# Two attentions, a norm and an MLP on one core: an earlier handed-over projection, and value weights scaled in place of the values

## The chip, the cores and the metric

The kernel runs on one core of one Trainium2 chip. The metric is the device time of one execution in microseconds (us); the time of before is a median of three runs. The engines are called as in the profile: PE is TensorE's matmul and PEld its weight load, DVE is VectorE, ACT is ScalarE, POOL is GpSimd, SP is the engine whose queue issues most of the transfers. PSUM, where matmuls write, has eight banks of 512 fp32 values for each of 128 partitions.

## The reference

Sixteen images with 256 channels and 32 x 32 positions pass through two layers. All is fp32.

```python
# layer 0: 4 heads of 64
xs = x.reshape(B, C, S).transpose(0, 2, 1)
q, k, v = jnp.split((xs @ w_proj + b_proj).reshape(B, S, 4, 192), 3, axis=-1)
attn = softmax(einsum('bihd,bjhd->bijh', q, k) * 64 ** -0.5, axis=2)
x = einsum('bijh,bjhd->bihd', attn, v).reshape(B, S, 256) @ w_out + b_out + xs
...
# layer 1: 8 heads of 32
def attention(x, qkv_w, proj_w, proj_b, phys_bias):
    ...
    attn = softmax(einsum('bhnd,bhmd->bhnm', q, k) * 32 ** -0.5 + phys_bias)
    out = einsum('bhnm,bhmd->bhnd', attn, v)
    return out @ proj_w.T + proj_b
x = x + attention(group_norm(x, gn1_w, gn1_b), qkv_w, proj_w, proj_b, phys_bias)
h = gelu(mlp_w1 @ group_norm(x, gn2_w, gn2_b) + mlp_b1, approximate=False)
return x + mlp_w2 @ h + mlp_b2
```

The group norm has 32 groups of 8 channels. `phys_bias` is one number per head, so it multiplies the exponentials of a head by exp(bias).

## The kernel before

**Stages.** The loop over the 16 images (`b`, called batch) runs, for each, a first attention (`attention_a`, names ending in `_a`), the first group norm (`g`), a second attention (`attention_b`, names ending in `_b`), the second group norm (`h`) and the MLP. The stages of neighbouring images are laid into each other by hand: the first half of the MLP of image b-1 (`hidden`) stands behind the first attention of image b; the second half (`outputs`) and the query, key and value products of image b+1 are pieces (`fill`) between the steps of the second attention of image b. The first image has no MLP beside it, and the last one no next image.

**Order.** The program is written as one sequence. `run` goes through a stage that is a generator, and calls `later.tick()` at each of its steps; `later.after(n, fn)` puts `fn` n ticks ahead. From this sequence the framework builds one queue per engine. An engine takes its queue in order; the order on VectorE and ScalarE isn't that of the source text in all places, since the framework may put an operation ahead of others that it finds independent.

**First attention.** Four items (two halves `t` of the positions, two channel halves `c`) of eight key blocks make 32 units. A unit n has the scores `s_a` (L390, into a double-bank slot), the exponential `e_a` on ScalarE (L398), and two units later the weighted sum `acc_a` (L411) and, from an item's second key block on, one addition `es_a` on VectorE (L423) for the denominators. At an item's end ScalarE and VectorE empty `acc_a` (L427, L428). Of the eight banks six form three slots 0, 1, 2, given out by `wide` to the least recently used first; two are single (`bank` 0 and 1). An item of odd number keeps its `acc_a` in slot 2, and `kept` holds that slot back from `wide`; an item of even number uses the single banks.

`normalise(t)` follows some ticks behind the second item of a half: it takes a slot, multiplies the sums by ones (`den_a`, L442), copies the result (L350), spreads it over the partitions by a DMA, inverts it (L359), sends it back by DMAs and has `res_a` multiplied (L468).

**What is handed over.** The last projection `j` of the second attention of image b-1 is not issued there but kept in `handed`. In `attention_a` of image b it is issued at the end of `normalise(0)`, between the scores of units 18 and 19 (numbered from 0):

```python
            kept.discard(2)
            if t == 0 and handed:
                handed.pop()()
```

`out_proj` writes `j` into a slot, adds it into `x` (L663), and takes statistics (L666). `group_norm` follows through `later`: `means` (L711, L713), three ticks on `variances` (a tiny matmul `gm_h`, L703 or L336, and L720 to L726), two ticks on `apply` (`gv_h`, L733, a power on GpSimd at L734, L736 to L740, and four steps `gn_h` at L746), and then, one tick each, five sums of the MLP's input (L875 to L879). The statistics of the second norm in a 64-column tiling are read by two halves of the partitions; the two tiny matmuls write the two banks of one slot.

**End of the first attention.** Behind the last unit come the first projection half `o` in bank 0, the denominators of the second half (`normalise(1)`) and `o` in bank 1, then `hidden` (L898, L911, L923 to L954), in the middle of which the other `o` and the first norm stand.

**Second attention.** Before it, five pieces: four query/key tiles `qk_b` and the first value tile `v_b`, each into a slot through `single` (a bank if `aside` names one); ScalarE copies `qk_b` (L770). VectorE copies `v_b` while it multiplies by `eones`, exp(bias) for each column (L793). Its 16 steps have two key blocks each: scores (L524), of which the first two tiles go to bank 0 and 1, five exponentials (L539), additions on VectorE (L555), and the weighted sum of the step before in bank 0 (L576). The second value tile goes to bank 0 in the first step's fill (`early`).

**Start of the program.** SP's queue loads the first half of `x`, its second half, then `wo`, `wq` (the weights of the second attention's q, k and v), `wpj`, and the next `x`. ScalarE makes exp(bias) (L205) and VectorE spreads it to `eones` (L206). A bias tile `bqk` is turned by TensorE and copied by VectorE (L1058); the copies of the first attention's q and k on ScalarE (L772) need it.

Of the kernel before, what the change touches and what calls it, by code (L numbers as in the profile page):

```python
# [14 lines left out]
P = 128  # L15
# [3 lines left out]
HEADS1, D1 = 8, 32  # L19
# [35 lines left out]
def kernel(  # L55
# [21 lines left out]
    nc = tc.nc  # L77
# [126 lines left out]
    def exp_bias():  # L204
        nc.scalar.activation(ebias, pb, AF.Exp)  # L205
        nc.vector.tensor_copy(eones, ebias.unsqueeze(2).to_broadcast([P, HEADS1, D1]))  # L206

    bvo = const.tile([P, CC], F32, name="bvo")
    m2b2 = const.tile([P, CC], F32, name="m2b2")

# [2 lines left out]
    with ExitStack() as first:  # L213
        first_pass(
            first, tc, x, out,
            dict(
                wp=wp, bqk=bqk, pb=pb, bo=bo, g1w=g1w, g1b=g1b, g2w=g2w,
                g2b=g2b, pjb=pjb, m1b=m1b, m2b=m2b, wo=wo, wq=wq, wpj=wpj,
                m2b2=m2b2, gavg=gavg, mhalf=mhalf, ones=ones, eones=eones,
                bvo=bvo, at_start=at_start, load_rest=load_rest, exp_bias=exp_bias,  # L220
                make_blocks=make_blocks,
                in_range=in_range,
            ),
        )

    good = nc.values_load(in_range[0:1, 0:1], min_val=0, max_val=1)
    with tc.If(good == 0):
        with ExitStack() as again:
            general_pass(
                again, tc, x, out,  # L230
                dict(
                    wp=wp, bqk=bqk, pb=pb, bo=bo, g1w=g1w, g1b=g1b, g2w=g2w,
                    g2b=g2b, pjb=pjb, m1b=m1b, m2b=m2b, wo=wo, wq=wq, wpj=wpj,
                    mlp_w1T=mlp_w1T, mlp_w2T=mlp_w2T, gavg=gavg, mhalf=mhalf, b_proj=b_proj,
                ),
            )


def first_pass(ctx, tc, x, out, k):
# [136 lines left out]
    def attention_a(b, qT, kT, v, project):  # L376
# [57 lines left out]

        def normalise(t):
            half = TB // 2
            den = wide(f"den_{key}_{t}")[:, 0, :]
            for c in range(CC):
                for g in range(2):
                    for h in range(2):  # L440
                        j = (2 * g + h) * 32
                        nc.tensor.matmul(  # L442
                            den[j : j + 32, c * half : (c + 1) * half],
                            k["ones"],
                            sums[t * CC + c][:, g, h * half : (h + 1) * half],
                            start=True,
                            stop=True,
                        )

            home = act.tile([P, CC, S], F32, tag="k1", name=f"d_{key}_{t}")  # L450
            denominators(
                f"{key}_{t}", den, home[:, 1, :TB], home[:, 0, : CC * TB],
                (2, 5) if t < NT - 1 else (1, 1),
                lambda full: scale(t, full),
            )


            kept.discard(2)
            if t == 0 and handed:
                handed.pop()()  # L460

        def scale(t, full):
            r = res[:, :, t * TB : (t + 1) * TB]
# [10 lines left out]
        for n, u in enumerate(units):  # L474
            pending.append(scores(*u))
            if n == len(units) - 1:
                break
            if n >= lag:
                weigh(*pending.pop(0))
            yield  # L480
        while pending:
            weigh(*pending.pop(0))
# [207 lines left out]
    def group_norm(key, src, stats, gw, gb, tag, out_tile, wait, then=None):  # L690
        st = {}

        def averages(name, src):
            if cols[0] == P:
                ps = bank(name, 1)
                product(ps[:, :CC], k["gavg"], src, start=True, stop=True)
                return [(slice(0, P), ps[:, :CC])]
            ps = wide(name)  # L700
            halves = [slice(h, h + HALF) for h in range(0, P, HALF)]
            for n, sl in enumerate(halves):
                nc.tensor.matmul(  # L703
                    ps[sl, n, :CC], k["gavg"][sl, sl], src[sl], start=True, stop=True
                )
            return [(sl, ps[sl, n, :CC]) for n, sl in enumerate(halves)]

        def means():
            mv = small.tile([P, CC, 2], F32, tag="mv", name=f"mv_{key}")
            for cc in range(CC):  # L710
                nc.vector.bn_aggr(mv[:, cc, :], stats[:, cc].rearrange("p t k -> p (t k)"))  # L711
            mean_c = small.tile([P, CC], F32, tag="mean_c", name=f"mean_c_{key}")
            nc.vector.tensor_copy(mean_c, mv[:, :, 0])  # L713
            st.update(mv=mv, mean_c=mean_c)
            later.after(wait, variances)

        def variances():
            mean = small.tile([P, CC], F32, tag="mean", name=f"mean_{key}")
            for sl, ps in averages(f"gm_{key}", st["mean_c"]):
                nc.vector.tensor_copy(mean[sl], ps)  # L720

            dv = small.tile([P, CC], F32, tag="dv", name=f"dv_{key}")
            nc.vector.tensor_sub(dv, st["mean_c"], mean)
            nc.vector.tensor_mul(dv, dv, dv)
            tv = small.tile([P, CC], F32, tag="tv", name=f"tv_{key}")
            nc.vector.tensor_add(tv, dv, st["mv"][:, :, 1])  # L726
            st.update(mean=mean, tv=tv)
            later.after(1 if cols[0] == P else 2, apply)

        def apply():  # L730
            rstd = small.tile([P, CC], F32, tag="rstd", name=f"rstd_{key}")
            for sl, ps in averages(f"gv_{key}", st["tv"]):
                nc.vector.tensor_scalar(rstd[sl], ps, EPS, None, ALU.add)  # L733
            nc.gpsimd.tensor_tensor(rstd, rstd, k["mhalf"], ALU.pow)  # L734
            a = small.tile([P, CC], F32, tag="ga", name=f"ga_{key}")
            nc.vector.tensor_mul(a, rstd, gw)  # L736
            ma = small.tile([P, CC], F32, tag="gma", name=f"gma_{key}")
            nc.vector.tensor_mul(ma, st["mean"], a)
            c = small.tile([P, CC], F32, tag="gc", name=f"gc_{key}")
            nc.vector.tensor_sub(c, gb, ma)  # L740
            y = act.tile([P, CC, S], F32, tag=tag, name=f"gn_{key}")
            out_tile.append(y)
            for t in range(NT):
                sl = slice(t * TB, (t + 1) * TB)
                for cc in range(CC):
                    nc.vector.tensor_scalar(  # L746
                        y[:, cc, sl], src[:, cc, sl],
                        a[:, cc : cc + 1], c[:, cc : cc + 1], ALU.mult, ALU.add,
                    )
            if then:  # L750
                then(y)

        means()

    def qkv(key, D, src, weights, b_qk, v_scale, qT, kT, v_dst):
# [18 lines left out]
        def v(n):  # L776
            ps = single(f"v_{key}_{n}")
            for i in range(2):
                sb = 2 * n + i
                for cc in range(CC):  # L780
                    product(
                        ps[:, i * C : (i + 1) * C],
                        src[:, cc, sb * P : (sb + 1) * P],
                        weights(cc, 2),
                        start=(cc == 0),
                        stop=(cc == CC - 1),
                    )
            d = v_dst()[:, 2 * n : 2 * n + 2]
            ps = ps.rearrange("p (b h d) -> p b h d", b=2, d=D)
            if v_scale is None:  # L790
                nc.scalar.copy(d, ps)
            else:
                nc.vector.tensor_mul(  # L793
                    d, ps, v_scale.unsqueeze(1).to_broadcast([P, 2, C // D, D])
                )

        return (
            [
# [6 lines left out]
    def qkv_0(b, xb):  # L805
# [5 lines left out]
        def v():  # L811
# [4 lines left out]
        return (q, kk, v), qkv(  # L816
            f"a{b}", D0, xb,
            lambda cc, which: k["wp"][:, cc, which].rearrange("p h d -> p (h d)"),
            k["bqk"], None, q, kk, v,
        )  # L820

    def qkv_1(b, xn):
# [3 lines left out]
        return (q, kk, v), qkv(  # L826
            f"b{b}", D1, xn,
            lambda cc, which: k["wq"][:, cc, which * C : (which + 1) * C],
            None, k["eones"], q, kk, lambda: v,
        )  # L830

    def attention_0(b, qkv_tiles, xb, norm):
# [251 lines left out]
        nc.vector.tensor_add(k["bvo"], ps[:, :CC], k["bo"])  # L1084

    later.after(2, fold_bias)
    hidden, outputs = [], []
    last = NT * CC * SB // 2 - 1
    for b in range(B):
# [25 lines left out]

        run_pieces(qk[:n] + v[:1])
        def early(piece):
            aside.append(0)  # L1120
# [56 lines left out]
def general_pass(ctx, tc, x, out, k):  # L1177
# [23 lines left out]
    nc.gpsimd.dma_start(w1, k["mlp_w1T"].rearrange("(c p) n -> p c n", p=P))  # L1201
    w2 = act.tile([P, HC, C], F32, tag="w2", name="g_w2")
    nc.gpsimd.dma_start(w2, k["mlp_w2T"].rearrange("(c p) n -> p c n", p=P))
    pbs = small.tile([P, HEADS1], F32, name="pbs", bufs=1)
    nc.vector.tensor_scalar(pbs, k["pb"], float(D1) ** 0.5, None, ALU.mult)

# [260 lines left out]
```

## Time and profile before

| what | value |
|---|---|
| median of 3 runs | 3700.42 us (3700.16 to 3700.57) |
| span of the profiled execution | 3698.8 us (no other timing of this execution is given) |
| TensorE matmul busy | 3644.9 us, 99% |
| VectorE busy | 2688.2 us, 73% |
| ScalarE busy | 2118.4 us, 57% |
| GpSimd busy | 121.1 us, 3% |
| granted TensorE clock, mean | 0.999 |

The span runs from the first to the last instruction. Busy time is the union of an engine's instructions. Matmul records overlap, since four 32-column tiles or the like run at once, and their ends are modelled; so the distance between the starts of two groups says more than a group's length. A row of the timeline has start, length, engine, line, operation, tiles and count, and in brackets the idle time of the engine ahead of it with what ended it.

### The profile page before, as it was taken

Reading aid. Unit: us, or ns where it says so; the run is one execution under the profiler, and the core shown is the slowest. Engines: PE = TensorE matmul, PEld = TensorE weight load, DVE = VectorE, ACT = ScalarE, POOL = GpSimd, SP = SyncE. Lnnn points to the kernel's source line nnn. Section 1 sums busy time; section 2 is a strip of 40 time slices with the busy share of each in tenths; the row PEclk is TensorE's granted clock in tenths of the full one; section 3 lists DMA queues with packets and bytes.
Section 4 is the critical chain, followed back from the end, with each engine's and each line's share of the span. In section 5 each row is a group of like instructions: output and inputs, shape, how many; then the busy total and the mean of one; then the engine's idle time right before and its main releaser. Section 6 shows DMA issues by size and latency. Waiting matters only on the chain.

```text
span 3698.8 us, 79399 instructions
## 1 busy us (share of the span) xinstructions
PE 3644.9 (99%) x34221; PEld 1290.8 (35%) x34221; DVE 2688.2 (73%) x3486; ACT 2118.4 (57%) x2768; POOL 121.1 (3%) x266
## 2 busy tenths in 40 slices
PE   9999999999999999999999999999999999999999
PEld 4333333333333333333333333333333333333333
DVE  4686767767677776777777777787777877677777
ACT  4665646556565665646656465564655656556572
POOL 3000000000000000000000000000000000000000
PEclk9999999999999999999999999999999999999999
DMA  4000110101101011010110101001010010101100
GB/s 146 11 16 30 53 33 13 50 30 53 33 14 50 30 53 33 19 49 28 50 33 19 50 27 50 32 19 50 27 56 27 23 46 33 50 27 42 36 28 27
DMA packets 66548, 138.35 MB, mean 37 GB/s; under 512 B 35630, under 2 KB 36398, under 8 KB 61966
## 3 DMA queue, kind: packets, MB, share of 16 engines
q1 hardware_dynamic: 63116, 126.64, 10.7%
q8 instruction: 270, 4.42, 0.5%
q0 software_dynamic: 1328, 6.17, 0.5%
q14 instruction: 88, 0.72, 0.1%
q10 hardware_dynamic: 1746, 0.40, 0.1%
HBM read 111.17 MB, written 21.23 MB: 36 GB/s over the span
## 4 chain that ended last, share of the span: by engine, by line
PE 81%; DVE 14%; issue 3%; DMA 1%; ACT 1%; POOL 1%; SPq 0%; DVEq 0%; ACTq 0%
PE s_b L524 12%; PE acc_b L576 12%; PE m L336 10%; PE s_a L390 9%; PE acc_a L411 8%; PE m L898 6%; PE qk_a L336 6%; PE qk_b L336 5%; DVE es_a L423 4%; PE v_a L336 3%; PE j L336 3%; PE v_b L336 2%; PE den_b L598 1%; DVE g L954 1%; DVE es_b L555 1%
## 5 line engine op out<-in xcount | busy, mean ns | idle before, releaser
L539 ACT ACTIVATE e_b<-s_b 128x1024 f32<-128x1024 f32 (+1 forms) x1280 | 983.0, 864 | 151.0 <-PE s_b L524 151.0
L555 DVE TENSOR_TENSOR es_b<-es_b,e_b 128x1024 f32<-128x1024 f32 x768 | 899.1, 1218 | 217.3 <-ACT e_b L539 217.2
L398 ACT ACTIVATE e_a<-s_a 128x1024 f32<-128x1024 f32 x512 | 521.3, 1025 | 360.1 <-PE s_a L390 345.7
L524 PE MATMUL s_b<-q,k 32*64 32x512 f32 x8192 | 526.9, 601 | 9.8 <-DVE v L793 7.0
L390 PE MATMUL s_a<-q,k 64*64 64x512 f32 x4096 | 532.6, 593 | 1.1
L411 PE MATMUL acc_a<-e_a,v 64*64 64x512 f32 x4096 | 528.5, 589 | 0.0
L423 DVE TENSOR_TENSOR es_a<-es_a,e_a 128x1024 f32<-128x1024 f32 x384 | 471.0, 1226 | 58.4 <-ACT e_a L398 39.1
L576 PE MATMUL acc_b<-e_b,v 128*32 128x512 f32 x4096 | 493.8, 600 | 0.0
L336 PE MATMUL m<-g,w 128*32 128x512 f32 (+1 forms) x3320 | 404.3, 592 | 0.0
L524 PEld LDWEIGHTS s_b<-q,k 32*64 32x64 f32 x8192 | 166.1, 130 | 337.3 <-issue 127.7
L411 PEld LDWEIGHTS acc_a<-e_a,v 64*64 64x64 f32 x4096 | 161.9, 133 | 277.5 <-issue 236.1
L390 PEld LDWEIGHTS s_a<-q,k 64*64 64x64 f32 x4096 | 152.6, 133 | 278.1 <-issue 208.2
L898 PE MATMUL m<-gn_h,w 128*128 128x512 f32 x512 | 243.7, 604 | 5.7 <-DVE g L924 3.3
L589 DVE TENSOR_TENSOR res_b<-res_b,acc_b 128x512 f32<-128x512 f32 x192 | 131.6, 686 | 145.5 <-PE acc_b L576 145.5
L336 PE MATMUL qk_b<-gn_g,wq 128*32 128x512 f32 (+1 forms) x1280 | 235.7, 594 | 1.7
L576 PEld LDWEIGHTS acc_b<-e_b,v 128*32 128x32 f32 x4096 | 108.6, 109 | 358.2 <-ACT e_b L539 194.8
L336 PE MATMUL qk_a<-x,wp 128*32 128x512 f32 (+1 forms) x1856 | 233.5, 592 | 0.0
L336 PEld LDWEIGHTS m<-g,w 128*32 128x32 f32 (+1 forms) x3320 | 121.4, 112 | 262.3 <-issue 235.0
L954 DVE TENSOR_TENSOR g<-g,g 128x512 f32<-128x512 f32 x320 | 206.0, 680 | 4.0 <-ACT g L911 2.8
L898 PE MATMUL m<-hs,w 128*128 128x512 f32 x384 | 177.9, 592 | 0.1
L555 DVE TENSOR_TENSOR es_b<-e_b,e_b 128x1024 f32<-128x1024 f32 x128 | 150.6, 1217 | 0.0
L911 ACT ACTIVATE g<-g,m1b 128x512 f32<-128x512 f32 x128 | 92.1, 722 | 99.6 <-DVE g L938 72.7
(146 smaller groups left out, 2793.5 us busy)
## 6 DMA issues: line engine op xcount, KB each, us to landing
w<-w_kept SPq DMA_DIRECT2D x30, 1792.0 KB
d_a<-row_a SPq DMA_DIRECT2D x64, 256.0 KB
rd_b<-row_b SPq DMA_DIRECT2D x252, 64.0 KB
out_dram<-x SPq DMA_DIRECT2D x63, 256.0 KB
x<-in_x_dram SPq DMA_DIRECT2D x30, 512.0 KB
w_kept<-w_made POOLq DMA_DIRECT2D x2, 1792.0 KB, 7.1
w_made<-in_L_conv_mlp_w_dram POOLq DMA_DIRECT2D x8, 256.0 KB, 6.5
x<-in_x_dram SPq DMA_DIRECT2D x4, 256.0 KB
```

The source lines that it names most:

```text
L336: nc.tensor.matmul(o[sl], w[:, sl], r, **flags)
L390: nc.tensor.matmul(s[h : h + HALF, g, :], kT[g * D : (g + 1) * D, c, kb * P + h : kb * P + h + HALF], qT[g * D : (g + 1) * D, c, t * TB : ...
L398: nc.scalar.activation(e, s, AF.Exp, scale=float(D) ** -0.5)
L411: nc.tensor.matmul(accs[i][h][g * D : (g + 1) * D, :], v[h * HALF : (h + 1) * HALF, kb, c * 2 + g], e[h * HALF : (h + 1) * HALF, g, :], st ...
L423: nc.vector.tensor_add(sums[i], held[i] if kb == 1 else sums[i], e)
L524: nc.tensor.matmul(outs[g][h : h + HALF, :], kT[g * D : (g + 1) * D, c, k0 : k0 + HALF], qT[g * D : (g + 1) * D, c, t * TB : (t + 1) * TB] ...
L539: nc.scalar.activation(to, s, AF.Exp, scale=float(D) ** -0.5)
L555: ins = nc.vector.tensor_add(d, es[n % 2] if kb == 0 else d, es[n])
L576: nc.tensor.matmul(acc[g * D : (g + 1) * D, :], v[:, kb + m, c * G + g], es[2 * m + g // 2][:, g % 2, :], start=(m == 0), stop=(m == 1),)
L589: nc.vector.tensor_add(r, r, acc)
L898: nc.tensor.matmul(ps, blocks[1][number - 1][:, i * P : (i + 1) * P], inputs[b][number], start=first, stop=True, skip_group_check=not first,)
L954: (nc.vector.tensor_add if plus else nc.vector.tensor_sub)(d, d, gs[(*what, i)])
```

## The change

- `j` is issued at the end of the step n = 12 of the first attention (the 13th), between the scores of units 12 and 13, in banks 0 and 1. `gm_h` goes to the same two banks. `apply` comes five ticks behind `variances` in that tiling, not two.
- The denominators take the least recently used of slots 0 and 1, never slot 2.
- The value columns of `wq` are multiplied by `eones` once (`scale_v`, two VectorE instructions of 128 x 256, given to `later` eight ticks ahead); all `v_b` are then copied by ScalarE (L770's kind of copy, at the line of `v`). `eones` still weights the denominators.
- The first two `qk_b` tiles go to banks 0 and 1.
- `general_pass`, which runs only if a check of the denominators' range fails, loads `wq` again.

The built queues differ as follows. On VectorE the two multiplications of `wq` stand directly behind the making of `eones` and ahead of the copy of `bqk`. On ScalarE each first `v_b` copy stands behind the four `qk_b` copies and ahead of the load of the exponential's table, and the second one behind the first step's five exponentials. On TensorE and VectorE `j` and its steps move to the second item, the norm's small steps to the end of the second item and the start of the third, and the five sums to the third item, between its additions.

```diff
+    def scale_v():
+        for cc in range(CC):
+            wv = wq[:, cc, 2 * C :].rearrange("p (h d) -> p h d", d=D1)
+            nc.vector.tensor_mul(wv, wv, eones)
...
         def normalise(t):
             half = TB // 2
-            den = wide(f"den_{key}_{t}")[:, 0, :]
+            den = wide(f"den_{key}_{t}", next(m for m in order if m != 2))[:, 0, :]
...
             kept.discard(2)
-            if t == 0 and handed:
-                handed.pop()()
...
             if n >= lag:
                 weigh(*pending.pop(0))
+            if n == SB + 4 and handed:
+                handed.pop()(apart=True)
             yield
...
-        def averages(name, src):
+        def averages(name, src, apart):
...
-            ps = wide(name)
+            if apart:
+                ps = [bank(f"{name}_{n}", n) for n in range(2)]
+            else:
+                both = wide(name)
+                ps = [both[:, n, :] for n in range(2)]
...
-            for sl, ps in averages(f"gm_{key}", st["mean_c"]):
+            for sl, ps in averages(f"gm_{key}", st["mean_c"], True):
...
-            later.after(1 if cols[0] == P else 2, apply)
+            later.after(1 if cols[0] == P else 5, apply)
...
-            for sl, ps in averages(f"gv_{key}", st["tv"]):
+            for sl, ps in averages(f"gv_{key}", st["tv"], False):
...
-            d = v_dst()[:, 2 * n : 2 * n + 2]
-            ps = ps.rearrange("p (b h d) -> p b h d", b=2, d=D)
-            if v_scale is None:
-                nc.scalar.copy(d, ps)
-            else:
-                nc.vector.tensor_mul(
-                    d, ps, v_scale.unsqueeze(1).to_broadcast([P, 2, C // D, D])
-                )
+            nc.scalar.copy(
+                v_dst()[:, 2 * n : 2 * n + 2],
+                ps.rearrange("p (b h d) -> p b h d", b=2, d=D),
+            )
...
     later.after(2, fold_bias)
+    later.after(8, k["scale_v"])
...
+        aside.extend((1, 0))
         run_pieces(qk[:n] + v[:1])
...
+    nc.gpsimd.dma_start(k["wq"], k["qkv_wT"].rearrange("(c p) n -> p c n", p=P))
```

More of the change, by code (lines that the diff above doesn't have):

```diff
@@ L220 @@
                 bvo=bvo, at_start=at_start, load_rest=load_rest, exp_bias=exp_bias,
+                scale_v=scale_v,
                 make_blocks=make_blocks,
@@ L234 @@
                     mlp_w1T=mlp_w1T, mlp_w2T=mlp_w2T, gavg=gavg, mhalf=mhalf, b_proj=b_proj,
+                    qkv_wT=qkv_wT,
                 ),
@@ L703, in averages @@
                 nc.tensor.matmul(
-                    ps[sl, n, :CC], k["gavg"][sl, sl], src[sl], start=True, stop=True
+                    ps[n][sl, :CC], k["gavg"][sl, sl], src[sl], start=True, stop=True
                 )
-            return [(sl, ps[sl, n, :CC]) for n, sl in enumerate(halves)]
+            return [(sl, ps[n][sl, :CC]) for n, sl in enumerate(halves)]
         def means():
@@ L753, in group_norm, with qkv @@
         means()
-    def qkv(key, D, src, weights, b_qk, v_scale, qT, kT, v_dst):
+    def qkv(key, D, src, weights, b_qk, qT, kT, v_dst):
         def qk(ch, which, t):
@@ L818, in qkv_0 @@
             lambda cc, which: k["wp"][:, cc, which].rearrange("p h d -> p (h d)"),
-            k["bqk"], None, q, kk, v,
+            k["bqk"], q, kk, v,
         )
@@ L828, in qkv_1 @@
             lambda cc, which: k["wq"][:, cc, which * C : (which + 1) * C],
-            None, k["eones"], q, kk, lambda: v,
+            None, q, kk, lambda: v,
         )
```

## The prediction

> **What bounds the kernel now.** I read the page's first block, then TensorE's waits, then the timeline around each wait. TensorE is the bound.
>
> ```profile
> span 3698.8 us, 79399 instructions
> PE 3644.9 (99%) x34221; PEld 1290.8 (35%) x34221; DVE 2688.2 (73%) x3486; ACT 2118.4 (57%) x2768; POOL 121.1 (3%) x266
> ```
>
> TensorE is idle for 53.9 us, and the change removes no matmul, so that caps the visible gain. What ends the idle time (us in total, times, longest):
>
> ```profile
> PE den_a L442 <- DVE res_a L428: 28.1, 15, 1.9
> PE s_b L524 <- DVE v L793: 7.0, 16, 1.2
> PE m L898 <- DVE g L924: 3.3, 15, 1.0
> ```
>
> The first two are what the change touches. The end of a first attention (start, length, engine, line; the bracket is idle time):
>
> ```profile
> 724.32 0.69 DVE L878 TENSOR_TENSOR hs<-gn_h 128x512 f32<-128x512 f32 x1
> ...
> 730.32 7.86 DVE L423 TENSOR_TENSOR es_a<-es_a,e_a 128x1024 f32<-128x1024 f32 x6
> 735.04 1.92 PE L336 MATMUL o<-res_a,wo 128*32 128x512 f32 x16
> 738.10 0.68 DVE L428 TENSOR_TENSOR res_a<-res_a,acc_a 128x512 f32<-128x512 f32 x1
> 738.83 1.07 PE L442 MATMUL den_a<-es_a,ones 128*32 128x256 f32 x16 [1.87 <-DVE res_a L428]
> ```
>
> VectorE is late: norm and input sums (722.49 to 727.34) stand ahead of the additions, and six run back to back. The start of a second attention:
>
> ```profile
> 777.44 0.59 ACT L770 COPY q<-qk_b 128x512 f32<-128x512 f32 x1 [1.13 <-PE qk_b L336]
> 778.05 1.28 ACT L539 ACT_TABLE_LOAD   x1
> 779.17 0.69 DVE L793 TENSOR_TENSOR v<-v_b,eones 128x512 f32<-128x512 f32 x1 [4.92 <-PE v_b L336]
> 780.18 3.84 ACT L539 ACTIVATE e_b<-s_b 128x512 f32<-128x512 f32 x5 [0.85 <-PE s_b L524]
> 780.97 1.93 PE L336 MATMUL v_b<-wq,gn_g 128*32 128x256 f32 x32
> 784.55 1.97 PE L524 MATMUL s_b<-q,k 32*64 32x512 f32 x32
> ...
> 800.39 1.12 PE L524 MATMUL s_b<-q,k 32*64 32x512 f32 x16 [0.33 <-DVE v L793]
> ```
>
> The table load lies in the 0.85 us and more that ScalarE waits for scores; the last row is the wait on v. At the start of the program:
>
> ```profile
> 7.27 0.37 SPq L167 DMA_DIRECT2D wq<-in_L_conv_qkv_w_dram  x1
> 10.32 0.29 DVE L206 COPY eones<-ebias 128x256 f32<-128x256 f32 x1 [8.91 <-ACT ebias L205]
> 10.73 0.15 DVE L1058 COPY bqk<-bqk 128x6 f32<-128x6 f32 x1
> 10.92 1.27 ACT L772 ACTIVATE k<-qk_a,bqk 128x512 f32<-128x512 f32 x2 [0.63 <-DVE bqk L1058]
> ```
>
> **Part 1: projection and norm earlier, den outside slot 2 (15 batches).** Moved: 32 matmul records of j, two STT (0.74 us), two bn_stats (0.68), two aggregations, some ten small VectorE steps, POOL's power (0.70), four norm steps (1.92 together), five sums (0.61 apart). The step issues no DMA, and SP's order is unchanged; on POOL the power moves ahead of one isum (0.22 us, nobody waits).
> Zero is the first scores of unit 19 (710.31 in the rows). Before: den is wanted at 736.96 (738.83 - 1.87), that is 26.65; the last addition ends at 738.10, 27.8, and L428, whose read frees slot 2, at 738.78.
> After, TensorE: twelve units of 1.716 (s_a 722.91 to 724.63) and 0.09 for gv, then 5.45 as before (731.50 to 736.96): wanted at 26.15.
> After, VectorE in built order: e19 arrives at 2.2 (1.10 from scores to exp, exp 1.02); addition 1.24; rstd at 3.4, POOL and three small steps to norm 1.73 (720.76 to 722.49), so norm at 5.1; norm 1.83, to 7.0; es20 1.14; four sums 2.4, to 10.5; es21 1.15, last sum 0.6, to 12.25; es22 and es23 2.5, to 14.75; first addition of the last item 1.24, L428 0.61, L468 1.13, to 17.7; six additions 7.78 (730.32 to 738.10), to 25.5. That is 0.6 us before den is wanted. The inverse that now stands between rstd and ga waits for a spread that lands 3.72 us after den (705.88 to 709.60), at 2.9: in time; its rows go out 0.9 later than now, for a use (L468) at 16.6.
> So the 1.87 us go: 15 x 1.87 = 28.1 us. The other slot alone would leave about 1.2 (738.10 against 736.96); the rest is the move. j's banks are free: acc_0 is emptied about three units earlier, acc_2 comes six later.
> gv_h used to stand where only two score slots rotate, and the scores two later waited for rstd: s_a starts at 721.15, 1.17 after acc at 719.98, where 0.86 is usual. At its new place slot 2 rotates too: 15 x 0.31 = 4.7 us. qk_b's first two tiles in banks instead of a slot that the MLP's L939 has just freed: some 0.1 each, 1.2 us in all.
>
> **Part 2: v on ScalarE.** Removed: 64 VectorE steps of 0.69; added: 64 copies, for which v_a's copies (L791, 586 ns) are the row. In the 14 middle batches the score group at 798.95 took 2.49 to its successor at 801.44, where 1.90 is usual (784.55 to 786.45). ScalarE is free at 796.70 and v_b_3 ends about 797.2, so the copy is done by 797.9, before TensorE needs the tile: 14 x 0.59 = 8.3 us.
> But the first v copy now stands ahead of the table load in ScalarE's built order. It waits for v_b_0 as VectorE did (779.17): copy to 779.78, load to 781.08, so the first exp ends near 781.70, not 780.78. It frees the bank that v_b_1 needs at 780.97: 0.79 us of stall. v_b_1's copy then queues behind five exps that end 784.9; its bank is free at 785.43, and TensorE, after v_b_1 and qk_b, asks at 785.34: 0.09 more. Cost: 14 x 0.88 = 12.3 us.
> Here a rule speaks against the change. The row says 1.28 us for a load that begins 0.02 after the copy before it. The Trainium skill, "ScalarE: Activation LUTs", section "What ACT_TABLE_LOAD costs", adds a drain of some 1.38 us to each switch, 2.66 in all. With that, 15 x 1.38 = 20.7 us more would be lost. I take the row: no drain shows there.
> First and last batch have no query/key filler beside v_b_1, so its copy behind the exps costs 0.9 in the first and 1.7 in the last (copy plus load). But two later waits on a late VectorE v (1.16 and 2.27 us longer groups) go. Walking four units with ScalarE's 3.84 for five exps: 2.2 gained in the first. In the last the half clock after that stall goes too, 3.0. Sum 5.2.
>
> **Part 3: value weights scaled at the start.** The built VectorE order puts the two multiplications of wq between eones and bqk; they wait for wq's DMA. Its 256 packets of 3072 bytes run from 9.87 to 14.04 us in the trace's packet list, behind wo on the same queue. Two 128x256 multiplications at about 0.3 (the eones row, 0.29) and the reduction put bqk at 15.0 instead of 10.73. ScalarE's first k copy is queued behind that, its slot is wanted by TensorE's fourth product at 12.3 (10.58 + 1.72) and free at about 15.95: 3.7 us of stall, with nothing beside it.
> Does the clock fall as well? Granted clock is the seventh entry, after five busy times:
>
> ```profile
> 3540.00:3543.20 3.20, 1.99 (x28) 0.29 (x19) 3.19 (x4) 2.92 (x4) 0.00 (x0) 1.00 0.00 0
> 3543.20:3546.70 3.50, 3.50 (x20) 0.93 (x24) 0.00 (x0) 1.02 (x1) 0.00 (x0) 0.51 0.00 0
> ```
>
>
> Half the clock is granted for 3.5 us after a stretch with 1.2 us of idle. The Trainium skill, "TensorE: Matmul & The Clock Gate", Part 1, "What's actually happening", asks for at least one idle window of some 3.4 us; 3.7 us of stall would rarely hold a whole one, and cost nothing more. By the row it falls: 3.4 us at half speed, 1.7 us. I take the row for a 3.7 us stall; the 1.87 us waits show that short ones mostly don't do it.
>
> **Sum.** Gained: 28.1 + 4.7 + 1.2 + 8.3 + 5.2 = 47.5. Lost: 12.3 + 3.7 + 1.7 = 17.7. Net 29.8 us. The profiled execution has no timing of its own beside its span of 3698.8, which lies 1.6 below the median of 3700.4; against the span this gives 3669.0, against the median 3670.6 us.
>
> **Costs with two ends.** v copy before a table load, which before never shows for v: from nothing (if the load need not wait) to 0.88 + 1.38 a batch; value 0.88, by the two rows. Wait for wq: 1.7 us of stall at the least (its queue had moved 1.11 MB by 12 us, and wo and wq are 1.05), 5 at most if the landing lags its last packet; value 3.7. den: from none to 1.2 us left, if VectorE is not sooner than in the rows; value none, with 0.6 us to spare. The idle waits that stay (m on g, 3.3 us) could shift by a slot either way; value 0, since after den the slots are handed round in the same order. Reloading wq in the general pass isn't executed; one DMA instruction more.
>
> **Rivals.**
> 1. The table load costs what the rule says: 29.8 - 20.7 = 9 us gained, 3691. For: first copy and load become serial fifteen times. Against: the 0.02 us between copy and load.
> 2. VectorE is not relieved enough: the move is six units for j but only about four for the norm, and es20 to es23 now stand behind it. If half of each den wait stays, 14 us less: 3685. Against: the chain above, with 0.6 us to spare.
> 3. Load and wq wait are both hidden: 29.8 + 12.3 + 5.4, so 3653. For: ScalarE has 0.85 us of idle time there. Against: that idle time ends at the scores, whereas the load would begin 1.7 us later than now.
> 4. Slower: in a middle batch v_b_1's copy waits behind five exps and holds bank 0, which the next scores need. Its place is the second unit of the second attention; it decides from (47.5 - 5.4) / 14 = 3.0 us a batch (the first and last batch's small share set aside), and beyond 3.5 the whole is slower by over 0.2%. At the longest it would be all of the exps and the copy, 3.84 + 0.59 = 4.4, so 14 x 4.4 - 42.1 = 19.5 us slower, 3720. Against: v_b_1 (1.75) and qk_b (1.83) run meanwhile and leave 0.09.
> 5. The norm does not come earlier at all, because VectorE orders it late again: den stays, only the slot's 0.7 us is won, 28.1 - 10.5 = 17.6 less: 3688. Against: the built order has the last sum ahead of es_a_2's sixth step, and not after its seventh.
>
> **Chances.** Forecast 0.66; rival 1 0.08, rival 2 and 5 together 0.13, rival 3 0.07, slower 0.06. 0.2% is 7.4 us, about what a measurement of this kernel can tell from no change. All but the slower case lie below 3693, rival 1 close to it, so 0.05 of it goes to no change: faster 0.89, same 0.05, slower 0.06. The forecast's own bounds (no load exposed: 3658; den half left and a longer start: 3686) and rivals 2, 3 and 5 give the range 3654 to 3689.
>
> **What the profile after would show.** den_a's wait on L428 gone from TensorE's list, and the last es_a addition ending before o does. No wait of s_b on a VectorE v. New: v_b_1 idle some 0.8 us on ScalarE's e_b in each batch but the first, with copy, load and exp in a row before it. At about 12.3 us a stall of 3 to 4 us on ScalarE's k, VectorE's wq step beginning after 14, and a clock of half in the next 3.4 us. VectorE 44 us less busy, ScalarE 37 more. The prediction is wrong if den waits as long as now (VectorE's queue was not the cause), if the drain shows between copy and load, or if TensorE's total idle time does not fall from 54 to between 20 and 35 us.

## The result, and the profile after

The changed kernel takes 3666.07 us (median of 4 runs, 3664.81 to 3666.70), the kernel before 3700.29 in the runs beside it: a ratio of 0.9908, 95% interval 0.9894 to 0.9922. That is 34.2 us less; the prediction was 29.8 less, 3670.6, with a range of 3654 to 3689. The profiled execution of after took 3666.7 us, 1.8 above its span.

The first block of the page of after (span, then busy time by engine):

```profile
span 3664.9 us, 79373 instructions
PE 3632.6 (99%) x34221; PEld 1346.2 (37%) x34221; DVE 2658.1 (73%) x3424; ACT 2154.3 (59%) x2832; POOL 129.5 (4%) x266
```

TensorE's idle time went from 53.9 to 32.3 us (3664.9 - 3632.6). But its busy time fell too, by 12.3 us, though it has the same 34221 matmuls. So more than a third of the gain is not in the idle time at all. The reason is in how a row is made: the ends of matmuls are modelled, so part of a short wait is drawn as a longer matmul. Distances between starts show all of it, and I use them below.

What TensorE waits for after (us in total, times, longest):

```profile
PE v_b L344 <- ACT e_b L547: 10.2, 15, 0.7
PE qk_a L344 <- ACT k L784: 4.1, 1, 4.1
PE m L906 <- DVE g L932: 3.3, 15, 1.0
...
PE s_b L532 <- ACT v L800: 1.4, 2, 0.8
```

The two waits that led the list of before, den_a with 28.1 us and s_b on VectorE's v with 7.0, are gone. Two new ones stand at the top, and both were named ahead: the second value tile waits for the exponentials, and the first key copies wait at the start. The last row is what remains of v's copies, in the first and the last batch.

The end of a first attention, from the timeline of after (start, length, then engine, line and tiles):

```profile
726.05 7.86 DVE L431 TENSOR_TENSOR es_a<-es_a,e_a 128x1024 f32<-128x1024 f32 x6
...
732.71 1.92 PE L344 MATMUL o<-res_a,wo 128*32 128x512 f32 x16
...
733.83 0.68 DVE L436 TENSOR_TENSOR res_a<-res_a,acc_a 128x512 f32<-128x512 f32 x1
...
734.45 1.05 PE L450 MATMUL den_a<-es_a,ones 128*32 128x256 f32 x16
```

L436 starts when the last addition is done, at 733.83, and den_a starts at 734.45 without waiting: 0.62 us between them, where the prediction's chain gave 0.6. From o to den_a it is 1.74 us (732.71 to 734.45). Before it was 3.79 (735.04 to 738.83).

The start of a second attention after:

```profile
774.38 0.59 ACT L800 COPY v<-v_b 128x512 f32<-128x512 f32 x1 [1.14 <-PE v_b L344]
774.99 1.28 ACT L547 ACT_TABLE_LOAD   x1
776.28 3.84 ACT L547 ACTIVATE e_b<-s_b 128x512 f32<-128x512 f32 x5
...
776.93 1.93 PE L344 MATMUL v_b<-wq,gn_g 128*32 128x256 f32 x32 [0.68 <-ACT e_b L547]
```

Copy, load and exponential stand in a row. The copy ends at 774.97, the load begins 0.02 us later, and the first exponential starts 0.01 us after the load. TensorE pays in the last row.

The start of the program after:

```profile
10.69 0.34 DVE L206 COPY eones<-ebias 128x256 f32<-128x256 f32 x1 [9.28 <-ACT ebias L205]
13.87 0.76 DVE L212 TENSOR_TENSOR wq<-wq,eones 128x256 f32<-128x256 f32 x2 [2.84 <-DMA wq<-in_L_conv_qkv_w_dram]
14.55 0.28 DVE L187 TENSOR_REDUCE borrowed<-borrowed 128x16 f32<-128x128 f32 x1
14.74 0.15 DVE L1066 COPY bqk<-bqk 128x6 f32<-128x6 f32 x1
...
14.93 1.27 ACT L784 ACTIVATE k<-qk_a,bqk 128x512 f32<-128x512 f32 x2 [4.27 <-DVE bqk L1066]
15.67 10.32 PE L344 MATMUL qk_a<-x,wp 128*128 128x512 f32 x20 [4.12 <-ACT k L784]
```

Read it from the bottom: TensorE waits 4.12 us for ScalarE's k copies, these wait for bqk, and bqk stands behind the two multiplications, which wait for wq's transfer. Three windows of the same time (busy time with counts for PE, PEld, DVE, ACT and POOL, then the granted clock):

```profile
11.50:15.20 3.70, 0.06 (x1) 0.00 (x0) 1.22 (x5) 0.27 (x1) 1.03 (x2) 1.00 1.06 303
15.30:18.60 3.30, 2.93 (x4) 1.37 (x5) 0.00 (x0) 1.48 (x3) 0.19 (x1) 0.50 1.02 390
18.70:22.00 3.30, 3.30 (x9) 1.39 (x9) 0.00 (x0) 1.37 (x2) 2.34 (x2) 1.00 0.94 366
```

Behind the stall the clock is 0.50 for about 3.4 us in this execution, as the prediction took it.

**By stages.** Measured between the first starts of groups, in the two traces, one batch:

| stage (from, to) | before | after | times |
|---|---|---|---|
| program start, first s_a | 27.98 | 32.83 | once |
| s_a, first o | 60.22 | 60.22 | 15 |
| o, first m | 6.51 | 4.43 | 15 |
| last m group to first qk_b, first qk_b to v_b | 3.71 + 6.97 | 3.43 + 6.87 | 15 |
| first to second s_b tile group | 5.48 | 6.37 | 14 |
| second to fifth s_b tile group | 22.18 | 21.59 | 14 |

A batch in the middle fell from 228.58 to 226.44 us. The gain is in the third and fourth row, and the third row has most of it.

### The profile page after: what moved, and what is told of

Read it like the earlier page. It is cut to its first block, busy times and chain, and to the rows that moved or that the text cites. A ratio compares the mean times of both kernels' runs of the same rounds, so it can differ in the third digit from the quotient of the medians.

```text
span 3664.9 us, 79373 instructions
## 1 busy us (share of the span) xinstructions
PE 3632.6 (99%) x34221; PEld 1346.2 (37%) x34221; DVE 2658.1 (73%) x3424; ACT 2154.3 (59%) x2832; POOL 129.5 (4%) x266
## 4 chain that ended last, share of the span: by engine, by line
PE 91%; DVE 4%; ACT 3%; DMA 1%; issue 1%; SPq 0%; ACTq 0%; POOL 0%; DVEq 0%
PE s_a L398 12%; PE acc_b L584 12%; PE s_b L532 12%; PE acc_a L419 12%; PE m L344 10%; PE m L906 9%; PE qk_a L344 6%; PE qk_b L344 5%; PE v_a L344 3%; PE j L344 3%; PE v_b L344 2%; ACT e_b L547 2%; PE o L344 2%; PE den_b L606 1%; DVE g L962 1%
## 5 line engine op out<-in xcount | busy, mean ns | idle before, releaser
L398 PE MATMUL s_a<-q,k 64*64 64x512 f32 x4096 | 544.3, 593 | 0.0
L419 PE MATMUL acc_a<-e_a,v 64*64 64x512 f32 x4096 | 540.1, 589 | 0.0
L419 PEld LDWEIGHTS acc_a<-e_a,v 64*64 64x64 f32 x4096 | 187.9, 133 | 251.5 <-issue 218.4
L398 PEld LDWEIGHTS s_a<-q,k 64*64 64x64 f32 x4096 | 175.9, 133 | 246.7 <-issue 193.1
```

Source lines behind the costliest of these rows:

```text
L398: nc.tensor.matmul(s[h : h + HALF, g, :], kT[g * D : (g + 1) * D, c, kb * P + h : kb * P + h + HALF], qT[g * D : (g + 1) * D, c, t * TB : ...
L419: nc.tensor.matmul(accs[i][h][g * D : (g + 1) * D, :], v[h * HALF : (h + 1) * HALF, kb, c * 2 + g], e[h * HALF : (h + 1) * HALF, g, :], st ...
```

## The experiments

The first four start from the kernel before and make one part of the change each. The others start from the changed kernel. A kernel of before has 3699.5 to 3700.1 us in the runs beside them.

**1. The slot of den alone.**

```diff
-            den = wide(f"den_{key}_{t}")[:, 0, :]
+            den = wide(f"den_{key}_{t}", next(m for m in order if m != 2))[:, 0, :]
```

> Before with one edit: the denominators never take slot 2. Theory (VectorE is late, and slot 2 adds the emptying of acc_3 on top): den_a then waits for the last es_a addition, which ended at 738.10 where den was wanted at 736.96, so some 1.2 us are left of 1.87 in each of 15 batches: 15 x 0.68 = 10 us gained, 3690. Rival (the slot is the whole cause): the 1.87 us go, 28 us gained, 3672. Rival (the slot is nothing): no change.

Measured: 3685.64 us, ratio 0.9964 (0.9951 to 0.9978), 14 us less than before; each stage from o to m fell from 6.51 to 5.49. The wait changes its name in the list:

```profile
PE den_a L442 <- DVE es_a L423: 12.7, 15, 0.9
```

and the timeline of this kernel (VectorE's rows, then TensorE's) shows where in den_a it lies:

```profile
734.01 2.55 DVE L423 TENSOR_TENSOR es_a<-es_a,e_a 128x1024 f32<-128x1024 f32 x2
736.48 0.68 DVE L428 TENSOR_TENSOR res_a<-res_a,acc_a 128x512 f32<-128x512 f32 x1
...
735.15 0.61 PE L442 MATMUL den_a<-es_a,ones 128*32 128x256 f32 x8
736.62 0.64 PE L442 MATMUL den_a<-es_a,ones 128*32 128x256 f32 x8 [0.85 <-DVE es_a L423]
```

The first eight matmuls of den_a read the sums of the third item, which have long been there; only the other eight need the last addition. They would have started 0.43 us after 735.15 and start at 736.62, 0.14 after the addition is done at 736.48. So giving den_a another slot returns about half of the wait, and what is left is VectorE's lateness with the last addition. It gave 14 us and not the 10 expected, since half of den_a no longer waits at all.

**2. The move alone** (projection and norm at step 13, in single banks; den's slot, v and qk_b as before).

```diff
-            if t == 0 and handed:
-                handed.pop()()
...
+            if n == SB + 4 and handed:
+                handed.pop()(apart=True)
...
-            later.after(1 if cols[0] == P else 2, apply)
+            later.after(1 if cols[0] == P else 5, apply)
```

> Before with the projection j and the norm moved as in the change (13th step, single banks, five ticks to apply), and nothing else; the denominators may take slot 2 again. Theory (the move relieves VectorE): in the changed kernel the emptying of acc_3 ended at 734.51 and den began at 734.45, so some 0.1 us of wait is left in each batch; about 15 x 2.0 = 30 us gained, 3670. Rival (the slot choice is needed as well): a wait near 0.7 us stays, 10 us less gained, 3680. The norm's own 0.3 us wait goes, but two more changes of tiling beside j and den take it back (0 in sum).

Measured: 3669.52 us, 0.9922 (0.9909 to 0.9936), 30.1 us less. The den_a row is gone from TensorE's list; o to m is 4.58 us. The move is thus nearly the whole gain, and the slot adds only 0.15 us a batch to it (4.58 to 4.43), 2.2 us in all. VectorE is not less busy in this kernel (2696.0 us, against 2688.2): it does the same work earlier. And the stage from s_a to o is 60.22 us as before: gv_h's gain of 0.31 a batch isn't there.

**3. The banks of qk_b alone.**

```diff
+        aside.extend((1, 0))
```

> Before with one edit: the first two qk_b tiles go to banks 0 and 1. The prediction had 1.2 us for this. By the two traces the group of eight m matmuls ahead took 3.709 us before and 3.433 after, and qk_b 6.971 against 6.867: 0.38 us in each of 15 batches, 5.7 us gained, 3694.6. Rival (those 0.38 us came from VectorE's earlier norm work or from the slots' other order after den): 1 us or less.

Measured: 3693.14 us, 0.9984 (0.9978 to 0.9991), 6.5 us less. From the last m group to qk_b it is 0.27 us shorter and from qk_b to v_b 0.10, in each of 15 batches: 5.6 us. The profiled spans differ by 7.5 us. Most of the remainder is in the last batch, whose second to fifth tile groups took 22.46 us before and 20.76 here: the stretch at half clock that the prediction showed at 3543 us isn't in this kernel's trace (nor in that of experiment 2, with 20.76 as well).

**4. Values on ScalarE, with wq scaled at the start, alone.**

```diff
+            nc.vector.tensor_mul(wv, wv, eones)
...
-                nc.vector.tensor_mul(
-                    d, ps, v_scale.unsqueeze(1).to_broadcast([P, 2, C // D, D])
-                )
+            nc.scalar.copy(
```

> Before with v copied by ScalarE and the value weights scaled at the start, and nothing of the move, the slot and the banks. Theory: start 4.9 lost, 0.89 lost in 14 batches (copy ahead of the table load), 0.58 gained in 14 batches (no wait on VectorE's v), 2.6 and 3.4 gained in the first and last batch: 3.2 us slower, 3703.5. Rival (moving v is a gain by itself, since VectorE is the late engine): 10 us faster, 3690, with the den wait shorter than 1.87.

Measured: 3704.28 us, 1.0012 (1.0006 to 1.0019): 4.6 us more than before. Its waits:

```profile
PE den_a L450 <- DVE res_a L436: 28.2, 15, 1.9
PE v_b L344 <- ACT e_b L547: 10.2, 15, 0.7
PE qk_a L344 <- ACT k L780: 4.0, 1, 4.0
```

VectorE has 36.9 us less to do in this kernel, and den_a waits for it as long as before (28.1). Relief spread over the second attention does nothing for a queue that is late in the first. What the part gives and takes is as predicted: +0.89 and -0.58 us a middle batch, 5.5 at the start, and about 6 back in the first and last batch. This half of the change is a loss by itself. With the slot's 2.2 us beside the move, the parts make 30.1 + 2.2 + 6.5 - 4.6 = 34.2 us, the whole gain.

**5. The scaling of wq on GpSimd** (from here on the changed kernel is the base).

```diff
-            nc.vector.tensor_mul(wv, wv, eones)
+            nc.gpsimd.tensor_mul(wv, wv, eones)
```

> The changed kernel with the two multiplications of wq on GpSimd, not VectorE. Theory (VectorE's queue held bqk behind wq's transfer): the stall of 4.1 us at 11.5 us goes, and with it the half clock of the next 3.4 us: 4.9 us gained, 3661. Rival (the clock falls for another reason): 4.1 gained at most, or 3.2, with the half clock still there. Rival (the stall is wq's or x's transfer itself): no change.

Measured: 3662.67 us, 0.9900 (0.9883 to 0.9917). The timeline of its start:

```profile
11.12 0.15 DVE L1066 COPY bqk<-bqk 128x6 f32<-128x6 f32 x1
...
11.31 1.26 ACT L784 ACTIVATE k<-qk_a,bqk 128x512 f32<-128x512 f32 x2 [0.65 <-DVE bqk L1066]
...
16.23 1.41 POOL L212 TENSOR_TENSOR wq<-wq,eones 128x256 f32<-128x256 f32 x2
```

bqk no longer waits for a transfer. The first scores start at 28.14 us, not 32.83, and the clock is full in all three windows. So the queue order was the whole cost of the start, 4.7 us between these two traces. The time is only 3.4 less, since in this trace the MLPs of the second and third batch took 0.5 and 0.6 us longer (28.95 and 30.45 against 28.45 and 29.85 from m to qk_b); these two early stages vary from kernel to kernel, and why wasn't settled.

**6. The table loaded before the first copy of v.** A tiny exponential ahead of the first v_b copy, in all batches but the first, puts the load where ScalarE has nothing to do.

```diff
-        run_pieces(qk[:n] + v[:1])
+        run_pieces(qk[:n])
+        if b:
+            hot = small.tile([P, CC], F32, tag="hot", name=f"hot_{b}")
+            tc.keep_in_program_order(nc.scalar.activation(hot, k["mhalf"], AF.Exp))
+        run_pieces(v[:1])
```

> The changed kernel with an exponential of 128x2 constants put between the qk_b copies and the first v_b copy on ScalarE (from the second batch on), so that the table's load stands ahead of that copy. Theory (the load, serial behind the copy, delays the first exp and so the bank of v_b_1): v_b_1's 0.68 us wait on e_b and the 0.14 us after it go: 0.89 x 15 = 13 us gained, 3653. Rival (the copy itself, not the load behind it, is too much for ScalarE there): 5 us or less gained. Rival (a load costs 2.66 us with its drain): then the first exp would be late again, and no gain.

Measured: 3656.13 us, 0.9885 (0.9868 to 0.9901). Its timeline at the same place:

```profile
769.49 1.28 ACT L1131 ACT_TABLE_LOAD   x1
...
770.78 0.20 ACT L1131 ACTIVATE hot<-mhalf 128x2 f32<-128x2 f32 x1
770.89 0.57 ACT L800 COPY v<-v_b 128x512 f32<-128x512 f32 x1
771.63 3.84 ACT L547 ACTIVATE e_b<-s_b 128x512 f32<-128x512 f32 x5 [0.17 <-PE s_b L532]
772.53 1.93 PE L344 MATMUL v_b<-wq,gn_g 128*32 128x256 f32 x32
```

The load lies in the time in which ScalarE waited for v_b, the exponentials wait for the scores again, and v_b has no wait. The step from first to second tile group is 5.61 us in place of 6.37: 0.76 of the 0.89 come back, 14 times. The cover is thin, with 0.17 us of idle time left ahead of the exponentials; the other 0.13 us weren't followed further. In time 9.9 us were gained, where 13 were expected. The profiled execution is the fastest of the four (3652.75, the others 3656.09 to 3657.88), and its start, whose code is the changed kernel's, is 1.9 us shorter than there (first scores at 30.97, not 32.83), at a place that the edit doesn't touch.

**7. The clock at the start.** Five matmuls of zeros put ahead of the product that stalls, so that TensorE isn't idle there; they take no part in the result.

```diff
-    run_pieces(start[2:])
+    start[2]()
+    keep_warm(nothing, 5)
+    run_pieces(start[3:])
```

> The changed kernel with five matmuls of zeros more on TensorE during its stall at the start. They are of no use to the result. Theory (the half clock follows from the idle time): the clock stays full, the stall on k stays, 1.7 us gained, 3664.4. Rival (the half clock has nothing to do with it, as with a rule of a whole idle window): the half clock comes all the same, no gain.

Measured: 3666.2 us, 0.9911 (0.9894 to 0.9927): as the changed kernel, 3666.07. Each of the five leaves two records: six ran from 9.84 us on, ahead of bqk's product, and four from 14.48 us on, where the stall was. The trace shows the clock at 1.00 in all three windows and the first scores 1.05 us sooner (31.78). That fits a half clock that follows from the idle time, but it is one trace, and the start without the zeros doesn't always bring the half clock: it came behind stalls of 4.1 and 4.0 us (the changed kernel, experiment 4) and not behind stalls of 2.6 and 2.9 us (experiments 6 and 9). The time doesn't give its price either: of the changed kernel's four executions only the profiled one has a mean clock of 0.999, the others 1.000, so most of them may not have had the stretch. In this trace the span is 0.8 us shorter; the MLP stage of the second batch was 1.5 us longer here and that of the third 1.4 shorter, so a gain of one microsecond can't be told in the time.

**8. Experiments 5 and 6 together.**

> The changed kernel with both: scaling on GpSimd and the table's load ahead of the first v_b copy. Theory: the two gains lie in different places and add up: 4.9 + 13 = 18 us gained on the changed kernel, 3648. Rival (one takes up the other, or ScalarE becomes the next bound): 3655 or more.

Measured: 3650.18 us (3649.62 to 3650.38), 0.9867 (0.9850 to 0.9883). This is the best version, 15.9 us below the changed kernel. The two faults of the change's second part are repaired by where an instruction stands, not by less work: TensorE's wait of 10.2 us on e_b has gone, and that of 4.1 us on k has shrunk to 0.6.

**9. The hand-over two units later.**

```diff
-            if n == SB + 4 and handed:
+            if n == SB + 6 and handed:
```

> The changed kernel with the hand-over two units later (SB + 6 in place of SB + 4); nothing else is changed. Theory (VectorE's lateness against den sets the wait, and the slack at step 13 is 0.62 us, from the last addition's end at 733.83 to den's start at 734.45): two units are two of the steps that TensorE makes in front of the additions, VectorE ends about 0.84 us later against den, so a den wait of 0.2 to 0.3 us comes back, 15 times: 3 to 4 us, about 3670 us, and den_a <- DVE is in the list of waits again. Rival: the slack is more than it looks since the additions simply move with the work, and any place before step 20 is as good: 3666 us, no den wait. Rival: the wait of the kernel before returns for the most part: 3685 us or more.

Measured: 3666.53 us, 0.9912 (0.9896 to 0.9929), not to be told from the changed kernel. The timeline of this kernel, again VectorE's rows and then TensorE's:

```profile
725.28 7.86 DVE L431 TENSOR_TENSOR es_a<-es_a,e_a 128x1024 f32<-128x1024 f32 x6
733.06 0.68 DVE L436 TENSOR_TENSOR res_a<-res_a,acc_a 128x512 f32<-128x512 f32 x1
...
732.72 1.11 PE L450 MATMUL den_a<-es_a,ones 128*32 128x256 f32 x16
```

The additions did become later against den_a: they end at 733.06, 0.34 us after its start, where they ended 0.62 before it. That is 0.96 us of delay for two units; 0.84 was expected. But den_a hardly stops, for the reason that experiment 1 showed: its second half is due 0.43 us after its start, at 733.15. From den_a to the next o it is 0.93 us in place of 0.86, so 0.07 a batch, 1.0 us in all. The expectation missed since it set the last addition against the first matmul of den_a, not against the first that reads it. The true slack at step 13 is about 0.9 us: of a delay of 0.96 us den_a felt only 0.07.

## Why the prediction was right, point by point

The terms of its sum, against the distances between starts in the two traces:

| step of the prediction | predicted gain | measured |
|---|---|---|
| den's wait | 28.1 | 31.3 (15 x 2.085) |
| gv_h's wait | 4.7 | 0.0 |
| qk_b's first tiles in banks | 1.2 | 5.6 (15 x 0.374) |
| v's wait gone | 8.3 | 8.2 (14 x 0.585) |
| v's copy ahead of the table load | -12.3 | -12.5 (14 x 0.89) |
| first and last batch | 5.2 | 6.0 (2.58 + 3.41) |
| wq at the start, with the clock | -5.4 | -4.85 |
| sum | 29.8 | 33.8, of 33.9 between the spans |

The sum is nearer than its terms, and that is in part luck: the 4.7 us of gv_h that did not come are more than made up by 3.2 from den and 4.4 from qk_b's banks that the prediction didn't have.

**Den's wait** went for the reason given. The chain through VectorE's built order ended 0.6 us ahead of den; 0.62 was there. Experiments 1 and 2 part the two causes: the slot alone is worth 1.02 us a batch, the move alone 1.93, both 2.085. They don't add up, as one wait has two releasers, and the later one decides. The term was too small by 3.2 us, because its size was taken from the list (1.87). By starts, o to den_a was 3.79 us before and is 1.74 after: 2.05. The list counts from the modelled end of o's last matmul, 1.92 us after the start of o, which is 0.18 later than the next group could have begun. The other 0.03 is den_a's own distance.

**gv_h's wait** is the step that failed. The wait itself did go: the distance from acc_a to s_a behind gv_h was 1.17 and is 0.86, and gv_h's neighbours lost 0.11 more (0.92 to 0.86 and 0.91 to 0.86). But 0.42 came back elsewhere: the prediction counted only the wait that goes, and put at nothing what j and den_a cost beside their new neighbours. Experiment 2, with the move alone, has the same distances and the same 60.22. Before, den_a and j stood side by side (timeline of before):

```profile
704.91 1.04 PE L411 MATMUL acc_a<-e_a,v 64*64 64x512 f32 x8
705.88 1.07 PE L442 MATMUL den_a<-es_a,ones 128*32 128x256 f32 x16
706.77 3.62 PE L336 MATMUL j<-res_b,wpj 128*32 128x512 f32 x32
```

After, each stands alone among the 64*64 matmuls of the attention (timeline of after):

```profile
706.37 1.10 PE L419 MATMUL acc_a<-e_a,v 64*64 64x512 f32 x8
707.40 1.07 PE L450 MATMUL den_a<-es_a,ones 128*32 128x256 f32 x16
708.40 1.09 PE L398 MATMUL s_a<-q,k 64*64 64x512 f32 x8
```

In a run of such groups one follows the other in 0.86 us. Next to a 128*32 group the distances are longer. Around j alone, acc_a ahead of it now takes 0.97 and s_a behind it 0.91: 0.16 us for the new pair of changes, and j itself 0.03. den_a's neighbours cost more than before (acc_a 1.03 against 0.97, den_a 1.00 against 0.89), and the last acc_a before o takes 2.74, not 2.69. Together 0.42, and 60.22 stays 60.22. A rival, that j or den_a waits there for a bank, isn't what the rows point to. They show the weight loads (timeline of after, PEld and PE):

```profile
691.85 0.15 PEld L419 LDWEIGHTS acc_a<-e_a,v 64*64 64x64 f32 x4 [0.28 <-issue]
692.28 1.04 PE L419 MATMUL acc_a<-e_a,v 64*64 64x512 f32 x8
...
693.25 0.16 PEld L344 LDWEIGHTS j<-res_b,wpj 128*32 128x32 f32 x8 [0.81 <-issue]
693.25 3.64 PE L344 MATMUL j<-res_b,wpj 128*32 128x512 f32 x32
```

The first weights of acc_a, which follows a group of its own tiling, are loaded 0.43 us ahead of it, while the scores before it still run. Those of j are loaded only as j starts, though "issue" says that they waited for nothing that the profile shows. It is the same for s_a behind j (696.82), for den_a (707.40; its row names ScalarE's L435, which had ended at 706.52) and for s_a behind den_a (708.40). Before, when j followed den_a, its first weights came 0.21 us ahead (706.55 for 706.77). So most of the 0.42 stands where a weight load isn't ahead of its group; for 0.11 of it (the rise from 0.97 to 1.03, and from 2.69 to 2.74) no row gives a reason. No experiment changes the tiling alone, so this cause is read from the rows and not tested.

**qk_b's banks** were right in kind and too small by 4.4 us. The prediction took "some 0.1 each, 1.2 us in all". Experiment 3 alone gives 0.37 in every one of 15 batches. TensorE's list of before has no row for it, but the list of its weight loads names it (one batch of before, then all batches of after):

```profile
PEld qk_b L336 <- DVE g L939: 0.9, 1, 0.9
...
PEld qk_b L344 <- DVE g L947: 7.2, 30, 0.2
```

qk_b's first load was held for 0.94 us (14.1 us in 15 batches) until L939 had freed the slot; after, the gaps ahead of its loads are 0.24 us, as usual. The distances have the cost: 3.71 us for the last eight matmuls of m (766.56 to 770.27 in the timeline of before), where the same eight take 3.43 after (762.16 to 765.59).

**v on ScalarE** was right to 0.2 us in both directions. Experiment 4 has the same numbers with nothing else changed, and experiment 6 shows that the load's place is the cause. Of the two prices the row decided: 1.28 us, and 0.02 us of gap. The Trainium skill's drain of 1.38 us ("ScalarE: Activation LUTs", "What ACT_TABLE_LOAD costs") doesn't show, and with it rival 1 falls: 9 us would have been gained, not 34. Rival 3, both costs hidden, is refuted by the two waits at the top of the list; experiments 5 and 6 had to move instructions to come near its 3653.

**First and last batch** gave 6.0 us, of which 1.7 are chance. They are the half clock at 3543 us: with it the second to fifth tile groups of the last batch took 22.46 us in the trace of before, and without it 20.76 in experiments 2 and 3, which leave v as it was. Not every execution has it. Of the 41 executions of before beside experiments 1 to 4, 20 have a mean clock of 1.000 and a median of 3698.6 us, and 21 have 0.999 and 3700.4.

**The start** was predicted as 3.7 us of stall and 1.7 for the clock, and came to 4.85 in the trace of after. The stall was 4.12, since TensorE's first products had started some 0.9 us sooner than before and bqk was at 14.74, not 15.0. With the clock's 1.7 that makes 5.8, and the sooner start gives 0.9 of it back. Of the half clock the prediction took the case's own row and not the Trainium skill's window of some 3.4 us ("TensorE: Matmul & The Clock Gate", Part 1, "What's actually happening"). The start can't tell the two apart: stalls of 4.1 us (after) and 4.0 (experiment 4) were followed by half clock, those of 2.6 and 2.9 us (experiments 6 and 9) were not, and both rules allow that. In those last two traces, with no other change at the start, the first scores came at 30.97 and 31.03 us, so the same code cost 3.0 us there, not 4.85. The stretch of before at 3543 us still speaks against the page's window, as it had 1.2 us of idle time; but the row isn't a rule either, since the same stage ran at full clock in experiments 2 and 3.

**The other side.** Rival 4's extreme, a bank held through all five exponentials in each middle batch, would have been 4.4 us a batch. 0.89 was paid, by a wait of 0.68 in the list. Rivals 2 and 5, a VectorE that is late again, are refuted by experiment 2.

Of what the profile after was to show, one point missed clearly: VectorE has 30.1 us less, not 44. The v steps account for 36.9 (experiment 4), and the move adds 7.8 (experiment 2); why it is 36.9 wasn't followed up. Three others are near: the stall is 4.1 us, not 3 to 4, the scaling of wq begins at 13.87 us, not after 14, and ScalarE has 35.9 us more, not 37.

## What to carry to other kernels

An engine can have a quarter of its time free and still set the end of a stage: what counts is how much stands ahead of the one instruction that is waited for. Follow that chain in the built order, with arrival times, down to the matmul that really reads its result. A list of waits doesn't show all of a wait: measure it by the distance between starts, against the same pair of groups where nothing waits, and look at the weight loads' waits too. And when work is handed to another engine, look for what it is put in front of there. Here one copy ahead of a table load and one multiplication behind a transfer took 15.9 us that a change of place alone gave back (experiment 8).

## What was unexpected of the hardware

At a change between 64*64 and 128*32 matmuls the distance between groups was longer by 0.05 to 0.17 us, though the list has no wait there: 0.91 for s_a behind j, 0.97 and 1.03 for acc_a ahead of j or den_a, where 0.86 is usual. The rows show one difference: behind a group of their own tiling the first weights were loaded ahead (0.43 us for acc_a), behind the other tiling only as the group started. Two groups of one tiling laid side by side were cheaper here than the same two apart, by about as much as the wait on gv_h that the move took away.

The half clock came in some executions of a kernel and not in others. A single trace with it or without it therefore says little about an edit, and 1.7 us can change sides between two traces.
